# Projected values in a graph kernel: shifted to their key places by the stores instead of by matmuls

## The chip, the cores and the metric

The kernel runs on one core of one Trainium2 chip. The metric is the device time of one execution in microseconds, the median of three runs; lower is better. TensorE (PE) does matrix products, VectorE (DVE), ScalarE (ACT) and GpSimd (POOL) work elementwise, and SyncE (SP) does nothing but issue transfers. Transfers issued by SP run on the queue q1, those issued by POOL on the queue q0; both use the same 16 DMA engines.

## The reference, cut to what matters

A graph of 3327 tokens with 128 features and a dense adjacency matrix `adj` (3327 x 3327) passes through four layers, each of them a message step, the residual sum and a layer norm. Only the first is touched here, an attention that uses `adj` as additive encoding:

```
n, d = x.shape                       # 3327, 128;  h = 8
q = (x @ Wq.T).reshape(d, n, h)      # the same for k and v
a = jnp.einsum('dnh,dmh->dnm', q, k) * scale
a = a + spatial_encoding + edge_encoding          # both are adj
a = jax.nn.softmax(a, axis=2)
out = jnp.einsum('dnm,dmh->dnh', a, v)
out = out.reshape(n, h * d)
return out @ Wo.T
```

There are 128 attention problems ("heads" d) with 3327 queries, 3327 keys and only 8 features. The reshape does not split features: it reads the projected matrix as one flat row. Value m of head d stands at flat place d * 3327 + m (in units of 8 numbers), so it comes from token (d * 3327 + m) // 128 and channel (d * 3327 + m) % 128. Because 3327 = 26 * 128 - 1, a key m = 128 * s + j of head d has channel (j - d) modulo 128 and token 26 * d + s, or one token less when j < d. The other three layers multiply `adj` (once also its transpose) with the features and are the same in both kernels.

## The kernel before, in words

The program has three parts.

The opening (lines 256 to 406, to some 300 us) projects the tokens. Tokens go in seven passes u of up to 512 (`SUPER`). `split` makes the query or key products of a pass on PE (`products`, L300, four groups of 128 tokens, 1024 columns each), cuts each number into a high part on ACT (L354) and a rest on DVE (L355), takes the largest on DVE (L357), and POOL stores both parts in the DRAM scratch `q_s` or `k_s` (L294). The tiles `hi` and `lo` have two buffers each, which queries and keys of a pass use in turn. Into the same loop go the transposes of later weights (`later_weights`) and, in passes 1 to 4, one row tile of the adjacency each (`ar`, loaded by SP at L89, its maxima on DVE at L403).

For the values, `values_projected` (L312) multiplies a pass of tokens by the value weights of each of the 8 features h: the result has one channel per partition and one token per column, and is copied by DVE and ACT in turn to `vp` (contiguous per h). Attention wants value m of a head on partition m % 128, and the channel is off by d. So `values_turned` (L321) handles two heads at a time: it multiplies the 26 tokens of the head by a 128-column window of `turn`, an identity with a zero block on each side; the window that starts at column 128 + r moves partitions by r, and a second product with the window at r brings in those that wrap around, from the next token. These products (L336) add up in PSUM, a strided copy (L159 on DVE, L157 on ACT, in turn) puts them in `vo`, and after 16 heads SP stores `vo` in the scratch `v_img` (L345) by four stores, one for each key block. `v_img` has 128 rows, one per partition of keys, and is laid out in each row by key block, then by group of four heads, head, token and feature, so that what attention loads at once is contiguous. `vo` shares its two buffers (tag `wide`) with the row tile `ar`.

Attention (L410 to 850, to some 9740 us) runs over 28 blocks, 7 of 476 queries by 4 of keys (7, 7, 6 and 6 tiles of 128 keys, `KBS`), and in each block over the 32 groups of four heads. PE makes the scores (L737), ACT their exponentials (L742) and, for a fixed share, DVE by a polynomial (L631 to L641); PE weighs the values (L777). The order on PE, ACT, POOL and DVE is written out by a planner in Python with costs per step; SP's order, and that of all engines in the opening, is the framework's. At the start of group n, `prepare` loads values for group n + 1 (`load_values`, L543) and queries and keys for group n + 2 (`load_heads`, L485). Every second call of `load_values` brings the values of two groups by one SP transfer (`vs`, L547); each call has POOL spread them (L551) into one of three padded tiles `v_pad`, 32 columns for 8 features. The products with these values come while the scores of group n + 2 are made.

The last part (from L1142) makes the other three layers and reads the attention result from the scratch `o_s` (L1255, 128 x 9 runs of 512 bytes each).

Of the kernel before, what the change touches and what calls it, by code (L numbers as in the profile page):

```python
# [10 lines left out]
F32 = mybir.dt.float32  # L11
# [8 lines left out]
P = 128  # L20
GROUP = 4
PACK = 3
SUPER = 512
# [28 lines left out]
def kernel(ctx: ExitStack, tc: tile.TileContext, x, adj, wq, wk, wv, wo,  # L52
# [14 lines left out]
    nc = tc.nc  # L67
    N, D = x.shape
    HD = wq.shape[0]
    H = HD // D  # L70
    T = (N + P - 1) // P
# [23 lines left out]
    def flat_ap(dram, at, pattern):  # L95

        f = dram.rearrange("r c -> (r c)")
        if isinstance(at, int):
            base = f[at:at + 1]
        else:  # L100
            base = f[ds(at, 1)]
        return bass.AP(base.tensor, base.offset, pattern)

    const = ctx.enter_context(tc.tile_pool(name="const", bufs=1))
    scratch = ctx.enter_context(tc.tile_pool(name="scratch", bufs=1, space=DRAM))

    ident = const.tile([P, P], F32, name="ident")
# [5 lines left out]
    q_s = scratch.tile([2 * H, RS], F32, name="q_s")  # L113
    k_s = scratch.tile([2 * H, RS], F32, name="k_s")

    v_img = scratch.tile([P, T * HD], F32, name="v_img")

    o_s = scratch.tile([A1, SLOTS], F32, name="o_s")

# [35 lines left out]
    def copy(i, dst, src):  # L155
        if i % 2:
            nc.scalar.copy(dst, src)  # L157
        else:
            nc.vector.tensor_copy(dst, src)  # L159
# [96 lines left out]
    with tc.tile_pool(name="pw", bufs=1) as pw, tc.tile_pool(name="pa", bufs=2) as pa, \  # L256
# [3 lines left out]
        def spread(u):  # L260
            base = u * SUPER
            n = min(SUPER, N - base)
            R = (n + P - 1) // P
            return base, R, n // R, n % R

        xT = pw.tile([P, NU, 4, P], F32, name="xT")
        xN = pw.tile([P, NU * SUPER], F32, name="xN")
        wqT = load_by_h(pw, ppw, wq, "wqT")
        for u in range(NU):
# [4 lines left out]
            for a, n in ([(0, P)] if full == P else [(0, 112), (112, full - 112)]):  # L274
                nc.sync.dma_start(out=xr[a:a + n, 0:R, :],
                                  in_=flat_ap(x, (base + R * a) * D, [[R * D, n], [1, R * D]]))
            if rest:
                nc.sync.dma_start(out=xr[full:full + 1, 0:rest, :],
                                  in_=flat_ap(x, (base + R * full) * D, [[D, 1], [1, rest * D]]))
            ps = pps.tile([P, 4, P], F32, tag="ps", bufs=3, name="xtr")  # L280
# [4 lines left out]
            if u == 0:  # L285
                wkT = load_by_h(pw, ppw, wk, "wkT")
                wvT = load_by_h(pw, ppw, wv, "wvT")
# [9 lines left out]
        def products(u, r, w):  # L297
            pp = pps.tile([P, HD], F32, tag="pp", name="pp")
            for c in range(0, HD, 512):
                nc.tensor.matmul(pp[:, c:c + 512], lhsT=xT[:, u, r, :], rhs=w[:, c:c + 512], start=True, stop=True)  # L300
            return pp.rearrange("p (h j) -> p h j", h=H)
# [2 lines left out]

        turn = pw.tile([P, 3 * P], F32, name="turn")
        nc.gpsimd.memset(turn, 0.0)
        nc.gpsimd.tensor_copy(turn[:, P:2 * P], ident)
        vp, vo = {}, {}  # L310

        def values_projected(u):  # L312
            n = spread(u)[1] * P
            vp[u] = pa.tile([P, H, SUPER], F32, name="vp")
            for h in range(H):
                ps = pps.tile([P, SUPER], F32, tag="ps", bufs=3, name="pv")
                nc.tensor.matmul(ps[:, 0:n], lhsT=wvT[:, h * D:(h + 1) * D], rhs=xN[:, u * SUPER:u * SUPER + n],
                                 start=True, stop=True)
                copy(h, vp[u][:, h, 0:n], ps[:, 0:n])

        def values_turned(d):  # L321

            g, i = d // 16, d % 16
            if i == 0:
                vo[g] = pa.tile([P, 4, T, 32], F32, tag="wide", name="vo")
            ps = pps.tile([P, 2, H, T], F32, tag="ps", bufs=3, name="vtr")
            for k in range(2):
                q, r = (d + k) * N // D, (d + k) * N % D
                for wrap in range(2 if r else 1):
                    at = q + wrap  # L330
                    while at < q + wrap + T:
                        u = at // SUPER
                        n = min(q + wrap + T, (u + 1) * SUPER) - at
                        s = at - q - wrap
                        first = (0 if wrap else P) + r
                        nc.tensor.matmul(ps[:, k, :, s:s + n], lhsT=turn[:, first:first + P],  # L336
                                         rhs=vp[u][:, :, at - u * SUPER:at - u * SUPER + n],
                                         start=(k == 0 and wrap == 0 and s == 0), stop=True,
                                         skip_group_check=True)
                        at += n  # L340
            copy(d // 2, vo[g][:, i // 4, :, i % 4 * H:(i % 4 + 2) * H].rearrange("p s (k h) -> p k h s", k=2), ps)
            if i == 14:
                for k0, nt in KBS:
                    w = nt * 32
                    nc.sync.dma_start(out=flat_ap(v_img, k0 * HD + g * 4 * w, [[T * HD, P], [w, 4], [1, w]]),  # L345
                                        in_=vo[g][:, :, k0:k0 + nt, :].rearrange("p g s c -> p g (s c)"))

        def split(u, w, s, top, f):
            hi = pa.tile([P, H, 4, D], F32R, tag="hi", name="hi")
            lo = pa.tile([P, H, 4, D], F32R, tag="lo", name="lo")  # L350
            R = spread(u)[1]
            for r in range(R):
                pp = products(u, r, w)
                nc.scalar.activation(hi[:, :, r, :], pp, AF.Copy, scale=f)  # L354
                nc.vector.scalar_tensor_tensor(lo[:, :, r, :], pp, f, hi[:, :, r, :].bitcast(F32),  # L355
                                               ALU.mult, ALU.subtract)
            nc.vector.tensor_reduce(top[:, u:u + 1], hi[:, :, 0:R, :].bitcast(F32), AX.XYZ, ALU.max,  # L357
                                    apply_absolute_value=True)
            store_slots(nc.gpsimd, s, 0, u, hi.bitcast(F32))
            store_slots(nc.gpsimd, s, H, u, lo.bitcast(F32))  # L360
# [25 lines left out]
            nc.sync.dma_start(out=klead_s[row:row + 1, :], in_=one)  # L386
        nc.sync.dma_start(out=k_s[:, SLOTS:RS], in_=zero[0:2 * H, :])

        d = 0
        for u in range(NU):  # L390
            split(u, wqT, q_s, top_q, SCALE / 2)
            split(u, wkT, k_s, top_k, 1.0)
            values_projected(u)
            if 2 <= u <= 4:
                later_weights(u - 2)
            last = u * SUPER + spread(u)[1] * P
            while d < D and (d + 1) * N // D + T < last:
                values_turned(d)
                d += 2
            if 1 <= u <= 4:  # L400
                ar = pa.tile([P, NP], F32, tag="wide", name="ar")
                load_rows(nc.sync, ar[:, 0:N], adj, u - 1)
                nc.vector.tensor_reduce(tops[:, u - 1:u], ar[:, 0:N], AX.X, ALU.max)  # L403
            if u == 4:
                store_tops(pw, 0, tops, P)
        assert d == D

    def attention():  # L410
        with tc.tile_pool(name="ed", bufs=1) as ed, tc.tile_pool(name="kq", bufs=3) as kq, \
# [131 lines left out]
            def load_values(b, g):  # L543
                k0, nt = KBS[blocks[b][1]]
                if g % 2 == 0:
                    pairs[b, g // 2] = kq.tile([P, 2, 7 * 32], F32, name="vs", bufs=2)
                    nc.sync.dma_start(out=pairs[b, g // 2].rearrange("p a c -> p (a c)")[:, 0:2 * nt * 32],  # L547
                                      in_=flat_ap(v_img, k0 * HD + g * nt * 32, [[T * HD, P], [1, 2 * nt * 32]]))
                vs = pairs[b, g // 2].rearrange("p a c -> p (a c)")[:, g % 2 * nt * 32:(g % 2 + 1) * nt * 32]
                vp = v_pads[(b * NHG + g) % 3]  # L550
                nc.gpsimd.tensor_copy(  # L551
                    vp[:, 32:32 + nt * GROUP * 32].rearrange("p (x c) -> p x c", c=32)[:, :, 0:H],
                    vs.rearrange("p (x c) -> p x c", c=H))
                return vp

            heads, values, pairs, edges, es, stores = {}, {}, {}, {}, {}, []
# [581 lines left out]
    wide = nc.values_load(flag[0:1, 0:1], min_val=0, max_val=1)  # L1138
# [27 lines left out]
    for i in range(4):  # L1166
        k = len(range(i, T, 4))
# [134 lines left out]
    with tc.manual_schedule(engines={mybir.EngineType.PE, mybir.EngineType.SP, mybir.EngineType.DVE}):  # L1302
# [21 lines left out]
        for t in range(T):  # L1324
            n = tokens(t)
            ps = gather(t, y1, 0, 6 + t % 2,
                        after(xs[1], t - 1, messages) if t else
                        [(2 + 5 * k, lambda k=k: stage0(T + k)) for k in range(4)])
            z = work.tile([P, D], F32, name="z")
            nc.vector.tensor_tensor(z[:n, :], ps[:n, 0:D], y1[:n, t, :], ALU.add)  # L1330
            h = work.tile([P, D], F32, name="h")
# [28 lines left out]
        for t in range(T):  # L1360
            n = tokens(t)
# [9 lines left out]
            ps = gather(t, y2, 0, 7 - t % 2, [(6, back)] + after(xs[0], t - 1, last_inputs))  # L1371
            h = work.tile([P, D], F32, name="h")
# [42 lines left out]
```

## Time and profile before

| | |
|---|---|
| time, median of 3 runs | 10480.76 us (10480.22 to 10483.09) |
| the profiled execution's own time | 10484.38 us |
| its span | 10482.6 us |
| PE, ACT, DVE, POOL busy over the span | 99%, 90%, 87%, 15% |
| transfers over the span | 2226.20 MB in 1017515 packets, mean 212 GB/s |
| 0 to 330 us: PE, DVE, ACT busy | 269.46, 190.60, 110.35 us |
| 0 to 330 us: the turning products L336 on PE | 97.52 us |
| first score product L737 | at 321.99 us |

The profile lists, for one execution, what each engine did and when. Groups of instructions carry the line of the kernel, the engine, the operation, the tiles written and read, the count, the busy time and the mean duration; a bracket behind a line of the timeline tells how long the engine had stood idle and what ended that. A matmul on 32-bit floats shows as two records. The table of stretches gives each engine's busy time in a window (with the number of instructions), TensorE's granted clock (1.00 is full speed), the mean busy share of the 16 DMA engines and the rate. The table of queues gives packets, megabytes and the time of the packets as a share of 16 engines over the window.

### The profile page before, as it was taken

The page shows a single profiled execution, that of the slowest core. Times are in us where ns is not written, and L with a number is a line of the kernel's source. Part 1 is how long each engine was busy: PE and PEld are TensorE (multiplying, and loading weights), DVE is VectorE, ACT ScalarE, POOL GpSimd, SP SyncE. Part 2 cuts the span into 40 slices and gives each one's busy share as a digit, 9 for nine tenths or more (in the row PEclk, how much of TensorE's full clock was granted, in tenths as well). Part 3 has the DMA queues.
Part 4 walks back from the last instruction along what each step waited for, and adds up shares of the span by engine and source line. Part 5 has one row for each costly group of instructions (what it writes and reads, how often), then busy time and mean ns, then how long its engine had stood idle before and what let it go on. Part 6 is the DMA issues. An engine that isn't in the chain of part 4 may idle for free. (4 is left out here: it accounts for less than half of the span.)

```text
span 10482.6 us, 208701 instructions
## 1 busy us (share of the span) xinstructions
PE 10365.6 (99%) x76835; PEld 4039.4 (39%) x76835; DVE 9079.7 (87%) x16616; ACT 9441.7 (90%) x11231; POOL 1525.6 (15%) x2733
## 2 busy tenths in 40 slices
PE   8899999999999999999999999999999999999999
PEld 5333333333333333333333333333333333333879
DVE  6789998899989999898998989989899988999722
ACT  3799999999999999999999999999999999999400
POOL 0111222111121111211112110111111210001200
PEclk9999999999999999999999999999999999999999
DMA  7766776666776667766676666666766766666786
GB/s 265 229 213 190 218 221 216 212 195 204 217 214 213 196 202 214 215 212 200 204 213 212 214 198 194 207 207 209 206 196 208 214 216 198 186 197 199 230 293 248
DMA packets 1017515, 2226.20 MB, mean 212 GB/s; under 512 B 195813, under 2 KB 720365, under 8 KB 1002671
## 3 DMA queue, kind: packets, MB, share of 16 engines
q1 hardware_dynamic: 935638, 2094.76, 65.4%
q0 software_dynamic: 79136, 116.02, 3.4%
q8 instruction: 621, 10.17, 0.4%
q14 instruction: 400, 3.28, 0.1%
q10 hardware_dynamic: 1720, 1.97, 0.1%
HBM read 1863.16 MB, written 348.72 MB: 211 GB/s over the span
## 5 line engine op out<-in xcount | busy, mean ns | idle before, releaser
L742 ACT ACTIVATE e<-sc 128x952 f32<-128x952 f32 (+2 forms) x10752 | 9220.3, 995 | 219.7 <-PE sc L737 144.7
L777 PE MATMUL o<-e,v_pad 128*32 128x476 f32 (+1 forms) x46592 | 5660.4, 573 | 2.7 <-DVE e L641 1.5
L737 PE MATMUL sc<-qt,kt 64*128 64x476 f32 x23296 | 4309.5, 436 | 28.8 <-DVE ey L631 15.4
L737 PEld LDWEIGHTS sc<-qt,kt 64*128 64x128 f32 x23296 | 2134.2, 184 | 4247.4 <-ACT e L742 2602.4
L641 DVE SCALAR_TENSOR_TENSOR e<-e,ey 128x476 f32<-128x476 f32 x4116 | 2643.7, 649 | 36.5
L631 DVE TENSOR_SCALAR ey<-sc 128x476 int32<-128x476 f32 x2058 | 1341.1, 652 | 587.5 <-ACT e L742 546.1
L777 PEld LDWEIGHTS o<-e,v_pad 128*32 128x32 f32 (+1 forms) x46592 | 1032.2, 108 | 1907.1 <-issue 1791.1
L551 POOL COPY v_pad<-vs 128x192 f32<-128x192 f32 (+1 forms) x896 | 438.1, 489 | 7850.1 <-PE o L777 5624.0
L641 DVE SCALAR_TENSOR_TENSOR e<-ey 128x476 f32<-128x476 f32 x2058 | 1333.1, 651 | 28.4
L641 DVE SCALAR_TENSOR_TENSOR e<-e,et 128x476 f32<-128x476 f32 x2058 | 1327.7, 648 | 7.6
L638 DVE TENSOR_SCALAR ey<-ey 128x476 int32<-128x476 int32 x2058 | 833.8, 408 | 15.0
L635 DVE TENSOR_SCALAR et<-ey 128x476 int32<-128x476 int32 x2058 | 832.9, 408 | 12.0
L242 POOL DMA_DIRECT2D adjT_s<-at x1352 | 755.1, 567 | 93.5 <-DMA adjT_s<-at 49.3
L1241 PE MATMUL bank<-y,eT 128*128 128x128 f32 (+1 forms) x4056 | 470.7, 275 | 0.4 <-DVE h L1373 0.4
L1241 PEld LDWEIGHTS bank<-y,eT 128*128 128x128 f32 (+1 forms) x4056 | 467.5, 192 | 3.3 <-DVE h L1373 0.6
L1195 ACT ACTIVATE rstd<-mv,eps 128x1 f32<-128x1 f32 x104 | 30.6, 295 | 268.6 <-DVE mv L1193 268.5
L537 DVE CAST qt<-qt 64x1904 fp32r<-64x1904 f32 x224 | 258.4, 1154 | 7.4
L791 DVE TENSOR_TENSOR acc<-o,acc 128x476 f32<-128x476 f32 x231 | 151.1, 654 | 106.2 <-PE o L777 104.7
L535 DVE TENSOR_SCALAR qt<-qt 32x1428 fp32r<-32x1428 f32 x224 | 205.9, 919 | 18.2 <-DMA qt<-lead_s 9.5
L799 POOL DMA_DIRECT2D o_s<-acc x304 | 182.8, 605 | 30.4 <-DVE acc L791 9.5
L1354 PE MATMUL bank<-a,y 128*128 128x512 f32 (+2 forms) x364 | 145.5, 562 | 0.0
L354 ACT ACTIVATE hi<-pp 128x1024 fp32r<-128x1024 f32 x52 | 53.1, 1025 | 89.8 <-PE pp L300 88.2
(142 smaller groups left out, 2231.8 us busy)
## 6 DMA issues: line engine op xcount, KB each, us to landing
qt<-qimg SPq DMA_DIRECT2D x672, 952.0 KB
kt<-k_s SPq DMA_DIRECT2D x5316, 96.0 KB
kt<-k_s SPq DMA_DIRECT2D x1762, 128.0 KB
qimg<-qt SPq DMA_DIRECT2D x224, 952.0 KB
eT<-adjT_s SPq DMA_DIRECT2D x78, 1664.0 KB
vs<-v_img SPq DMA_DIRECT2D x224, 224.0 KB
adjT_s<-at POOLq DMA_DIRECT2D x1352, 32.0 KB, 3.7
vs<-v_img SPq DMA_DIRECT2D x224, 192.0 KB
```

Of the source, the lines that this page charges most:

```text
L242: nc.gpsimd.dma_start(out=flat_ap(adjT_s, (t * P + 32 * q) * NP + c * PIECE, [[NP, 32], [P, ns], [1, P]]), in_=at[32 * i:32 * i + 32].rear ...
L535: return [(0.9, lambda: nc.vector.tensor_scalar(qt[32:64, 1:], qf[0:32, 0:GROUP - 1], -1.0, None, ALU.mult)), (0.42, lambda: nc.vector.ten ...
L537: (1.17, lambda: nc.vector.tensor_copy(qt[64:128], qf[0:64]))]
L551: nc.gpsimd.tensor_copy(vp[:, 32:32 + nt * GROUP * 32].rearrange("p (x c) -> p x c", c=32)[:, :, 0:H], vs.rearrange("p (x c) -> p x c", c=H))
L631: nc.vector.tensor_scalar(yi, x, -58 * math.log(2.0), 2 ** 24 / math.log(2.0), ALU.max, ALU.mult)
L635: nc.vector.tensor_scalar(parts["t"].bitcast(I32), yi, UPPER, EXPONENT, ALU.bitwise_and, ALU.bitwise_xor)
L638: nc.vector.tensor_scalar(yi, yi, LOWER, QUARTER, ALU.bitwise_and, ALU.bitwise_or)
L641: nc.vector.scalar_tensor_tensor(e, e if i else y, POLY[i], parts["t"] if i == len(POLY) - 1 else y, ALU.add, ALU.mult)
L737: nc.tensor.matmul(s[:, i, 0:CW], lhsT=kt[64 * rg:64 * rg + 64, k, pos * P:(pos + 1) * P], rhs=qt[64 * rg:64 * rg + 64, k, :], start=False ...
L742: nc.scalar.activation(e[:, 0:own, :], s[:, 0:own, 0:CW], AF.Exp, bias=-2 * PHASE, scale=2.0)
L777: nc.tensor.matmul(o[32 * j:32 * j + 32, 0:CW], lhsT=values[b, g][:m, c:c + 32], rhs=es[b, g * GROUP + j, r][:m, :], start=first and u == ...
L1241: nc.tensor.matmul(ps[:n, 0:D], lhsT=e[:m, s, :n], rhs=y[:m, s, col:col + D], start=(s == 0), stop=(s == T - 1))
```

## The change

The shifted identity, its products, `vp` by passes of 512 tokens and `vo` go. A pass of values now covers 19 heads (`SPAN`, the last one 14), that is 19 * 26 tokens and one more ahead of them, and `vp` holds token by token with the 8 features inside, so that the 26 tokens of one head are a contiguous run of 208 numbers in each partition. Two SP stores per pass carry these runs to `v_img`: partition p of head d goes to row p + d, and what wraps goes by the second store to row p + d - 128, taken from one token earlier. Each store takes whole sets of 32 partitions, so some runs are stored twice, once to a row outside the 128; for these `v_img` has a margin of 64 rows on both sides. The rows are now laid out by head, token and feature. A load of attention therefore takes eight separate runs per partition, one for each head, in place of one, and POOL's spreading copy swaps the order of heads and tokens. In the pass loop the values now stand ahead of the queries.

```diff
-    v_img = scratch.tile([P, T * HD], F32, name="v_img")
+    MARGIN, SPAN = 64, 19
+    v_img = scratch.tile([P + 2 * MARGIN, T * HD], F32, name="v_img")
...
-        turn = pw.tile([P, 3 * P], F32, name="turn")
-        nc.gpsimd.memset(turn, 0.0)
-        nc.gpsimd.tensor_copy(turn[:, P:2 * P], ident)
-        vp, vo = {}, {}
...
+        def values_projected(i):
+            d0 = i * SPAN
+            n = min(SPAN, D - d0)
+            at = T * d0 - 1
+            skip = 1 if at < 0 else 0
+            vp = pa.tile([P, SPAN * T + 1, H], F32, name="vp")
             for h in range(H):
                 ps = pps.tile([P, SUPER], F32, tag="ps", bufs=3, name="pv")
+                w = n * T + 1 - skip
+                nc.tensor.matmul(ps[:, 0:w], lhsT=wvT[:, h * D:(h + 1) * D], rhs=xN[:, at + skip:at + skip + w],
                                  start=True, stop=True)
-                copy(h, vp[u][:, h, 0:n], ps[:, 0:n])
-        def values_turned(d):
...
+                copy(h, vp[:, skip:skip + w, h], ps[:, 0:w])
+            row = T * HD
+            j = min(P, (P - d0 + 31) // 32 * 32)
+            nc.sync.dma_start(out=flat_ap(v_img, (MARGIN + d0) * row + d0 * T * H, [[row, j], [row + T * H, n], [1, T * H]]),
+                              in_=vp[0:j, 1:1 + n * T, :].rearrange("p (d s) h -> p d (s h)", s=T))
+            j = (P - (d0 + n - 1)) // 32 * 32
+            d = max(d0, 1)
+            nc.sync.dma_start(out=flat_ap(v_img, (MARGIN + j + d - P) * row + d * T * H,
+                                          [[row, P - j], [row + T * H, d0 + n - d], [1, T * H]]),
+                              in_=vp[j:P, (d - d0) * T:n * T, :].rearrange("p (d s) h -> p d (s h)", s=T))
...
-        d = 0
         for u in range(NU):
+            values_projected(u)
             split(u, wqT, q_s, top_q, SCALE / 2)
             split(u, wkT, k_s, top_k, 1.0)
-            values_projected(u)
...
-                    nc.sync.dma_start(out=pairs[b, g // 2].rearrange("p a c -> p (a c)")[:, 0:2 * nt * 32],
-                                      in_=flat_ap(v_img, k0 * HD + g * nt * 32, [[T * HD, P], [1, 2 * nt * 32]]))
+                    nc.sync.dma_start(
+                        out=pairs[b, g // 2].rearrange("p a c -> p (a c)")[:, 0:2 * nt * 32].rearrange("p (j c) -> p j c", c=nt * H),
+                        in_=flat_ap(v_img, MARGIN * T * HD + g * GROUP * T * H + k0 * H,
+                                    [[T * HD, P], [T * H, 2 * GROUP], [1, nt * H]]))
...
-                    vp[:, 32:32 + nt * GROUP * 32].rearrange("p (x c) -> p x c", c=32)[:, :, 0:H],
-                    vs.rearrange("p (x c) -> p x c", c=H))
+                    vp[:, 32:32 + nt * GROUP * 32].rearrange("p (t j c) -> p j t c", j=GROUP, c=32)[:, :, :, 0:H],
+                    vs.rearrange("p (j t c) -> p j t c", j=GROUP, c=H))
```

More of the change, by code (lines that the diff above doesn't have):

```diff
@@ L301, in products @@
             return pp.rearrange("p (h j) -> p h j", h=H)
-        turn = pw.tile([P, 3 * P], F32, name="turn")
-        nc.gpsimd.memset(turn, 0.0)
-        nc.gpsimd.tensor_copy(turn[:, P:2 * P], ident)
-        vp, vo = {}, {}
-        def values_projected(u):
-            n = spread(u)[1] * P
-            vp[u] = pa.tile([P, H, SUPER], F32, name="vp")
+        def values_projected(i):
[4 more added lines that the diff above has]
+            vp = pa.tile([P, SPAN * T + 1, H], F32, name="vp")
@@ L315, in values_projected @@
             for h in range(H):
                 ps = pps.tile([P, SUPER], F32, tag="ps", bufs=3, name="pv")
-                nc.tensor.matmul(ps[:, 0:n], lhsT=wvT[:, h * D:(h + 1) * D], rhs=xN[:, u * SUPER:u * SUPER + n],
+                w = n * T + 1 - skip
+                nc.tensor.matmul(ps[:, 0:w], lhsT=wvT[:, h * D:(h + 1) * D], rhs=xN[:, at + skip:at + skip + w],
                                  start=True, stop=True)
-                copy(h, vp[u][:, h, 0:n], ps[:, 0:n])
-        def values_turned(d):
[L323 to L346, printed above, removed]
@@ L387 @@
         nc.sync.dma_start(out=k_s[:, SLOTS:RS], in_=zero[0:2 * H, :])
-        d = 0
+        assert N == T * P - 1 and NU * SPAN >= D and SPAN * T < SUPER
         for u in range(NU):
+            values_projected(u)
             split(u, wqT, q_s, top_q, SCALE / 2)
             split(u, wkT, k_s, top_k, 1.0)
-            values_projected(u)
             if 2 <= u <= 4:
                 later_weights(u - 2)
[L396 to L399, printed above, removed]
             if 1 <= u <= 4:
@@ L405 @@
                 store_tops(pw, 0, tops, P)
-        assert d == D
     def attention():
```

## The prediction

> **What bounds the kernel now.** I read the page first, for the whole span, and then the stretches of the opening, because the change touches the opening and the loads of attention, and nothing else.
>
> ```profile
> span 10482.6 us, 208701 instructions
> PE 10365.6 (99%) x76835; PEld 4039.4 (39%) x76835; DVE 9079.7 (87%) x16616; ACT 9441.7 (90%) x11231; POOL 1525.6 (15%) x2733
> ```
>
> Attention, from some 322 us to 9740 us, is nine tenths of the span, and TensorE, ScalarE and VectorE are all nearly full there. The transfers are not: in the window from 5000 to 6000 us the queue table has
>
> ```profile
> q1 hardware_dynamic: 95431, 202.19, 66.9%
> ```
>
> so q1 takes two thirds of the 16 DMA engines' time. The opening looks different. The table of stretches of 20 us (busy time of PE, PEld, DVE, ACT, POOL, then granted clock, DMA share, GB/s):
>
> ```profile
> 80.00:100.00 20.00, 20.00 (x98) 16.91 (x97) 12.37 (x11) 7.05 (x8) 1.77 (x2) 1.00 0.96 348
> 120.00:140.00 20.00, 20.00 (x94) 16.64 (x93) 12.19 (x12) 6.94 (x8) 1.77 (x2) 0.91 0.76 279
> 160.00:180.00 20.00, 20.00 (x90) 15.48 (x89) 15.32 (x15) 7.82 (x9) 1.78 (x2) 0.97 0.77 286
> 200.00:220.00 20.00, 18.92 (x60) 11.30 (x61) 17.52 (x14) 6.68 (x9) 2.66 (x3) 0.86 0.50 184
> 220.00:240.00 20.00, 18.94 (x78) 13.19 (x77) 8.58 (x11) 7.46 (x12) 0.00 (x0) 1.00 0.95 329
> ```
>
> Neither PE nor the DMA engines are full throughout: they take turns. The timeline shows how. A run of 82 turning products holds PE for 14.5 us, the next query products come only behind it, and GpSimd, which issues the q and k stores, waits for them:
>
> ```profile
> 167.84 14.56 PE L336 MATMUL vtr<-vp,turn 128*128 128x208 f32 x82
> 192.47 0.89 POOL L294 DMA_DIRECT2D q_s<-hi  x1 [22.08 <-ACT hi L354]
> ```
>
> In slices of 5 us the DMA share then falls to 0.19 (165 to 170 us), 0.00 (210 to 215) and 0.25 (255 to 260), and is 1.00 or more in the slices in which two stores are queued (170 to 185). So the opening is bound by a chain: products, the store, a hole in the transfers while PE turns values.
>
> ```profile
> q0 software_dynamic: 12960, 50.32, 52.8%
> q1 hardware_dynamic: 18518, 22.49, 26.5%
> ```
>
> These are the queues from 46 us (the first k store) to 305 us, when the last value store has landed and attention's own loads and memsets start. 79.4% with the instruction queue's 0.1%: 259 x 0.794 = 205.7 us of full transfer, and 53 us of holes.
>
> **The change, part by part.**
>
> *Turning products gone.* L336 is busy 97.5 us (534 records); their 64 copies take 27.8 us of DVE and 28.2 us of ACT. PE in the first 330 us falls from 269.5 to 172 us. The memset and copy of the shifted identity (0.42 and 0.28 us on POOL near 1 us) lay beside the first loads: nothing.
>
> *Projected copies become strided.* The 56 projecting matmuls stay, 495 instead of 512 columns wide: nothing. Their copies write every eighth word. The contiguous 128x512 copy takes 683 ns on DVE, 583 ns on ACT; bounds for a strided one are these and the two strided rows, xN (16 bytes apart, 1084 ns on ACT for 512) and vo (128 bytes apart, 880 ns for 416, so 1047 for 495). I take 1.0 us, as both strided rows say: 28 x 0.32 = +9 us of DVE, 28 x 0.42 = +12 us of ACT, less than the vo copies that go. DVE ends at 172 us of 330.
>
> *Stores.* Before, 32 stores with 8 x 4 x 4 x 128 = 16384 packets of 896 or 768 bytes. After, 14 stores of 832-byte runs. Partitions times d over the seven passes give 3008, 3648, 3040, 3648, 3040, 3648 and 2240 packets, 22272 in all, since a partition between the two masks is stored twice, once into the margin. Price of a packet: from 86 to 100 us, q1, then almost only v_img, has
>
> ```profile
> q1 hardware_dynamic: 1316, 1.12, 24.9%
> ```
>
> 0.249 x 16 x 14 us / 1316 = 42.4 ns. So 16384 x 42.4 / 16 = 43.4 us becomes 59.0 us: +15.6 us. The new runs go to a different row of the scratch each, four of the old ones lay side by side; no row shows that. Bounds: 36 ns (832 bytes at the 23 bytes/ns of the 4096-byte stores, 168 ns each) gives +6.7 us, 59 ns (twice the 512-byte row below) +39 us. I take 42.4, the nearest in size and direction.
>
> *The end of the opening.* Work is 205.7 + 15.6 = 221.3 us of full transfer. Is there always a store ready? One pass of queries and keys in the fourth pass runs on PE from 139.57 to 167.84 us, 28 us, already with the projecting matmuls and with the wait for the adjacency row tile (VectorE idle 5.17 us before its maximum). The transfers of a pass: 2048 packets x 168 ns / 16 = 21.5 us for q and k, 8 to 10 us for values, 5 us for the row tile in passes 2 to 5: 31 to 36 us. So transfers become the bound, and the two hi and lo buffers are what is late next: q of the next pass waits until q of this one is stored. In stretches with stores queued the share is 0.95 to 0.96 (220 to 240, 80 to 100 us). 221.3 / 0.95 = 233 us instead of 259: **26 us earlier**. Bounds: share 1.00, 38 us earlier; the present 0.794, 20 us later, if the holes have another cause. Half-speed stretches of PE (granted clock 0.50 from 155 to 160 us) cost some 2.7 us at a restart (6.32 instead of 3.6 us for eight records); two a pass make 33 us of the 28, still within 36.
>
> On SP the value stores stand ahead of the row tiles and later weights. Four v_img issues took 3 to 9.5 us when q0 was full and eight took 32. The row tile waits behind, VectorE behind that with the lo parts, k's products behind those; it eats some of the 38 us. Against that, the row tiles no longer share buffers with vo, so the first two can load in the empty slices before 46 us (10 us of transfer). I let these two cancel.
>
> *Attention's value loads.* 448 loads, from 128 runs of 1792 or 1536 bytes to 1024 runs of 224 or 192 bytes. Issue on SP: before 0.38 us; the nearest row with as many runs (128 x 9 of 512 bytes, L1255) has 0.36 us, the v_img store with 512 runs 1.14 us. Queued behind it are one query and eight key loads for the second group ahead. Groups start 10.8 us apart, so 1 us more is covered by 21 us. Landing: POOL's copy waits for vs 172 times, but its product comes two groups later, so 20 us cover that too. Transfer: before 8 packets an engine at q1's mean of 112 ns (0.669 x 16000 / 95431), 0.9 us. After, 64 an engine, bounded by 9 ns (the 4-byte signals, too small) and 29.5 ns, from the o loads of 512 bytes at 9760 to 9780 us:
>
> ```profile
> q1 hardware_dynamic: 8923, 4.45, 82.3%
> ```
>
> 64 x 29.5 = 1.9 us, so +1.0 us per two groups (21.6 us): the share goes from 0.67 to 0.72, hidden. If that cover were gone, 448 us. The Trainium skill, "DMA: Bandwidth & Descriptors" (Specifications), says that transfers under 512 bytes fall below line rate because the engine then reads, modifies and writes. No run here shows that. At twice the 512-byte price the share would be 0.81 and the sum the same.
>
> *POOL's spreading copy.* 896 copies with as many elements; the output pattern has three loops instead of two, rows still of 8. 548 and 430 ns for 224 and 192 elements. Between nothing and a doubling; a gain has no reason. I take nothing, as cost follows elements (medians near 376 and 343 ns, 1 ns each). Where a copy lies beside VectorE, that loses: L638 took 0.58 us at 4999.87 beside a copy, 408 ns on the mean. The Trainium skill, "SBUF — State Buffer" (Who interferes with whom), says the two engines take a shared port pair in turn and the second blocks; the trace agrees with these 0.17 us.
>
> **Sum.** -26 + 0 + 0 = -26 us. The profiled execution took 10484.4 us (span 10482.6), 3.6 above the median; it goes to 10458, and the median 10480.8 to **10455 us**. About 0.2% (21 us) is what can be told from no change.
>
> **Rivals.**
> - *Full gain and more.* Row tiles load early and transfers never pause: 221.3 - 10 = 211 us, 48 us earlier, 10433 us. For it: empty slices before 46 us. Against: nothing fills 0 to 25 us better than now.
> - *Gain lost in the stores.* Scattered packets at 59 ns, or value stores that hold up the row tiles: (205.7 + 39) / 0.95 = 258 us, no change, 10480 us. For it: SP held 32 us by eight stores at 66 us. Against: 42 ns held even with q0 full.
> - *Slower: VectorE behind POOL.* If the three-loop copy takes twice as long, VectorE loses another 0.13 to 0.17 us 896 times, 134 us on the mean, in a stage where it is 92% busy. With two thirds on the path: +89 - 26 = +63, 10544 us. It ends slower from 47 us, 35% of the hits. For it: the 0.17 us. Against: same elements, VectorE's small reserve.
> - *Slower: short runs fill the queue.* It decides where 64 packets take 0.9 + 0.33 x 21.6 = 8 us, 125 ns each; at 130 ns attention gains 2% or so, 10650 us. Against: 29.5 ns for 512 bytes. The page's rule on short transfers points this way, and reaches less than half of it.
>
> **How the numbers follow.** Forecast 0.62 (own range 10440 to 10472; three quarters of it below 10460), more gain 0.08, lost gain 0.12, VectorE 0.14, queue 0.04. Faster: 0.47 + 0.08 = 0.55; same: 0.15 + 0.12 = 0.27; slower 0.18. The range takes in all but the two slower cases: 10430 to 10496.
>
> **What would show it.** Right: no vtr; DMA share 0.9 or more from 60 to 265 us; the first score product (now 321.99) near 296; q1 in attention at 0.70 to 0.75; POOL copies near 376 ns; attention's length as before. Wrong: vp copies or the copy on POOL much longer, packets of the value stores over 50 ns, holes in the transfers with VectorE waiting for the row tile, or attention longer by more than 20 us.

## The result, and the profile after

| | before | after |
|---|---|---|
| time, median (lowest to highest of 7 runs) | 10480.76 us (10479.1 to 10483.09) | 10444.85 us (10438.71 to 10451.84) |
| the profiled execution's own time, span | 10484.38, 10482.6 us | 10451.84, 10450.0 us |
| first score product | 321.99 us | 299.85 us |
| first score product to the last output store's issue | 10148.8 us | 10146.6 us |
| that issue to the end of the span | 11.8 us | 3.6 us |

The ratio is 0.9967, 95% interval 0.9958 to 0.9976: 35.9 us or 0.34% faster. The profiled execution of after is 7 us above its median, the slowest of its seven. Between the two profiles 32.6 us went: 22.2 in the opening, 2.2 in attention and the later layers, 8.2 at the very end.

The page of after, its first lines:

```profile
span 10450.0 us, 207506 instructions
PE 10285.0 (98%) x76301; PEld 3949.3 (38%) x76301; DVE 9060.6 (87%) x16584; ACT 9424.9 (90%) x11199; POOL 1519.5 (15%) x2731
```

PE lost 81 us of busy time, more than twice what the kernel gained. The same five stretches of 20 us as before (busy time of PE, PEld, DVE, ACT, POOL, then granted clock, DMA share, GB/s):

```profile
80.00:100.00 20.00, 16.90 (x33) 7.00 (x33) 12.81 (x10) 8.09 (x8) 1.77 (x2) 0.83 1.05 264
120.00:140.00 20.00, 17.40 (x35) 7.40 (x36) 12.90 (x11) 9.26 (x9) 1.77 (x2) 0.82 0.67 223
160.00:180.00 20.00, 5.30 (x9) 2.52 (x10) 7.55 (x4) 2.16 (x3) 0.89 (x1) 0.57 1.00 308
200.00:220.00 20.00, 15.51 (x35) 6.14 (x33) 16.24 (x10) 8.92 (x11) 3.54 (x4) 0.91 0.99 315
220.00:240.00 20.00, 10.14 (x17) 3.77 (x17) 9.56 (x7) 4.37 (x5) 1.77 (x2) 0.83 1.03 364
```

PE was busy through nearly all of each stretch; now it stands idle for up to three quarters of one, and the DMA engines are full in four of five. The queues from 46 to 305 us, the window that carried the prediction's 205.7 us of full transfer:

```profile
q0 software_dynamic: 13055, 50.65, 54.6%
q1 hardware_dynamic: 25872, 23.77, 34.7%
```

In attention, from 5000 to 6000 us, q1 moves the same bytes with half as many packets again, and its share hardly moves (66.9% before):

```profile
q1 hardware_dynamic: 139759, 202.79, 69.2%
```

One thing differs in the opening that is neither PE nor a store: the row tiles of the adjacency. By the tile `ar`, before and then after (durations are smallest, median, largest in ns; then first and last start):

```profile
L89 SPq DMA_DIRECT2D ar<-in_adj_dram x4: 346/346/346, 102.6 to 239.4; - x4
L403 DVE TENSOR_REDUCE tops<-ar x4: 3608/3619/3619, 109.7 to 247.6; 128x1 f32<-128x3327 f32 x4
```

```profile
L89 SPq DMA_DIRECT2D ar<-in_adj_dram x4: 352/392/422, 3.0 to 27.3; - x4
L382 DVE TENSOR_REDUCE tops<-ar x4: 3580/3608/3619, 10.0 to 63.3; 128x1 f32<-128x3327 f32 x4
```

All four are issued by 27.3 us instead of one a pass, and VectorE waits 2.0 us for them instead of 13.6. The old program gave `ar` and `vo` the same two buffers, so a row tile could load only when values had been stored; without `vo` nothing holds it. What that does to the transfers, by windows:

```profile
0.00:46.00 46.00, 30.64 (x87) 15.19 (x88) 22.37 (x30) 18.55 (x28) 4.79 (x13) 0.93 0.55 188
46.00:280.00 234.00, 214.00 (x770) 138.32 (x769) 154.20 (x123) 82.08 (x101) 22.32 (x27) 0.95 0.79 284
```

are of before, and

```profile
0.00:46.00 46.00, 30.50 (x74) 14.53 (x75) 28.38 (x28) 15.79 (x23) 3.25 (x10) 0.85 0.84 315
46.00:280.00 234.00, 148.78 (x311) 60.35 (x309) 138.42 (x101) 74.93 (x82) 26.94 (x33) 0.81 0.95 305
```

of after. The first 46 us were half empty and are now 0.84 full: (0.84 - 0.55) x 46 = 13.3 us of full transfer moved out of the stretch behind. So two explanations compete for the opening: the one predicted (PE's bursts opened holes), and the row tiles.

### The profile page after: what moved, and what is told of

The parts are those of the page before. It is cut to its first block, busy times and chain, and to the rows that moved or that the text cites. A ratio compares the mean times of both kernels' runs of the same rounds, so it can differ in the third digit from the quotient of the medians.

```text
span 10450.0 us, 207506 instructions
## 1 busy us (share of the span) xinstructions
PE 10285.0 (98%) x76301; PEld 3949.3 (38%) x76301; DVE 9060.6 (87%) x16584; ACT 9424.9 (90%) x11199; POOL 1519.5 (15%) x2731
## 5 line engine op out<-in xcount | busy, mean ns | idle before, releaser
L618 DVE TENSOR_SCALAR ey<-ey 128x476 int32<-128x476 int32 x2058 | 837.5, 410 | 14.9
L513 DVE TENSOR_SCALAR qt<-qt 32x1428 fp32r<-32x1428 f32 x224 | 205.4, 917 | 12.4 <-DMA qt<-q_s 6.7
```

The source lines that it names most:

```text
L618: nc.vector.tensor_scalar(yi, yi, LOWER, QUARTER, ALU.bitwise_and, ALU.bitwise_or)
```

## The experiments

Times are medians, ratios stand against runs of before on the same chip; "end" is the stretch from the last output store's issue to the end of the span, in the profiled run.

### Bursts and row tiles, one at a time

The first kernel is after with PE's bursts put back: about as many turning products as a pass of tokens used to have (256 in all, where before has 267), on data that is at hand, without their copies and without `vo`.

```diff
+            last = u * SUPER + spread(u)[1] * P
+            while heads_done < D and (heads_done + 1) * N // D + T < last:
+                ps = pps.tile([P, SUPER], F32, tag="ps", bufs=3, name="vtr")
+                for k in range(4):
+                    nc.tensor.matmul(ps[:, 0:208], lhsT=ident, rhs=xN[:, 208 * k:208 * k + 208],
+                                     start=True, stop=True)
+                heads_done += 2
```

> The changed kernel with PE's bursts put back alone: after the keys of a pass, for every two heads that were turned there before, four float32 products of 128x208 with the identity go into a PSUM tile that nobody reads (256 products, some 90 us of PE); no copies, no other stores. Theory (the bursts made holes in the transfers, and their removal is the gain): the opening gets 15 to 30 us longer again, 10460 to 10475 us. Rival 1 (the gain came from the row tiles of the adjacency, which no longer share buffers with vo) and rival 2 (from the 56 us of vo copies off VectorE and ScalarE): within 7 us of the changed kernel, 10438 to 10452 us.

The second is before, with one buffer for the row tile alone:

```diff
-                ar = pa.tile([P, NP], F32, tag="wide", name="ar")
+                ar = pa.tile([P, NP], F32, tag="ar", name="ar", bufs=1)
```

> The kernel before with one edit: the row tile ar has a buffer of its own, so its loads and maxima can run early; values are turned by products as before. Theory (bursts): the holes stay, only VectorE's 13.6 us of waiting for row tiles and some transfer time move: 3 to 15 us faster than before, 10466 to 10478 us. Rival 1 (row tiles): most of the gain, 10445 to 10455 us. Rival 2 (copies): as before, 10478 to 10484 us.

The third is after, with the row tile held back until the value copies of its pass. Its loads are then issued at 70.8 to 172.2 us, earlier than in before (102.6 to 239.4), but VectorE waits longer for them, 27.7 us where before waits 13.6:

```diff
                 ar = pa.tile([P, NP], F32, tag="wide", name="ar")
+                nc.vector.tensor_copy(ar[:, 0:1], vps[u][:, 1, 0:1])
```

> The changed kernel with the row tiles late again: VectorE first writes one word of ar that it reads from the vp of the same pass, so the load can start only then. Theory (opening now bound by transfers): 20 us of transfer go back into the full stretch, less the 7 us by which the first k store came later (52.0 instead of 44.7 us): 5 to 15 us slower than the changed kernel, 10450 to 10460 us. Rival 1 (row tiles are the gain): 10470 to 10480 us. Rival 2: 10443 to 10447 us.

Measured, with the fourth corner, which came last (both edits of after together):

> The kernel after with both edits: the dummy turning products (256 of 128x208) back on PE, and the row tiles held until the value copies of their pass. Alone, the first gave a first score product at 289.6 us, the second at 304.6 us; before, which has both, stands at 322.0, and with its row tiles freed at 303.2. Theory 1 (the bursts and the late row tile open the holes only together: a pass lasts longer than its 31 to 36 us of transfers only if PE's 14.5 us and VectorE's wait both lie in its chain): first score between 314 and 328 us, DMA share from 46 to 280 us below 0.88, time 10470 to 10490. Theory 2 (the late row tile alone makes them, bursts never cost anything): first score 300 to 308 as in the run with late row tiles alone, time 10460 to 10472. Theory 3 (bursts pay by a higher granted clock): 288 to 298 and 10440 to 10455.

| | time (us) | ratio to before | first score | end |
|---|---|---|---|---|
| before | 10481.86 | | 322.0 | 11.8 |
| before, row tiles early | 10455.92 | 0.9975 (0.9966 to 0.9985) | 303.2 | 3.6 |
| after, bursts back, row tiles late | 10473.62 | 0.9991 (0.9982 to 1.0) | 312.7 | 12.4 |
| after, row tiles late | 10468.02 | 0.9987 (0.9978 to 0.9996) | 304.6 | 11.7 |
| after, bursts back | 10439.5 | 0.996 (0.9946 to 0.9973) | 289.6 | 3.6 |
| after | 10444.85 | 0.9967 (0.9958 to 0.9976) | 299.8 | 3.6 |

The windows of, in turn, before with early row tiles, after with bursts back, after with late row tiles, and after with both:

```profile
0.00:46.00 46.00, 28.40 (x72) 13.78 (x73) 29.39 (x28) 15.35 (x23) 3.90 (x12) 0.87 0.80 299
46.00:280.00 234.00, 225.91 (x844) 150.59 (x842) 155.62 (x132) 90.64 (x113) 28.95 (x36) 0.98 0.79 277
```

```profile
46.00:280.00 234.00, 217.87 (x823) 144.70 (x821) 141.89 (x102) 75.68 (x80) 29.52 (x37) 0.97 0.93 312
```

```profile
0.00:46.00 46.00, 29.62 (x80) 14.39 (x81) 20.86 (x27) 16.77 (x25) 3.25 (x10) 0.89 0.54 187
46.00:280.00 234.00, 142.61 (x302) 59.02 (x300) 143.81 (x105) 74.27 (x80) 26.15 (x32) 0.81 0.95 323
```

```profile
0.00:46.00 46.00, 29.94 (x81) 14.03 (x82) 21.11 (x28) 17.08 (x25) 3.26 (x10) 0.85 0.55 187
46.00:280.00 234.00, 215.98 (x789) 142.28 (x789) 146.41 (x103) 74.89 (x80) 25.48 (x31) 0.96 0.91 314
```

What follows. The one-line change to before, with every turning product, copy and store left as it was, brings 25.9 of the 36 us, 8 at the end and 18 in the opening; its time is 0.9 us above the range for the row tiles and far from the other two. Holding the tiles late costs after 23.2 us (its 10468.02 lies between the ranges of the two theories), and 34.1 when the bursts are back; some 8 of that is the end, so 15 and 25 would be the opening. The first score products of the single profiles differ by 4.8 and 23.1 us, so the smaller of the two is not well known. The bursts cost 5.6 us with late row tiles and nothing (5.4 us the other way, ranges overlapping) with early ones. Kernels that are alike in bursts and in early or late tiles still differ by 16 us (before with early tiles against after with bursts back) or 8 us (before against the fourth corner): that is the copies, the new stores and the new order together, and none of these was tried alone. In the runs with late tiles the first 46 us are at 0.54 or 0.55 again.

The window of after with bursts back is the plainest answer to the prediction: PE busy for 218 of 234 us, and the DMA share is 0.93 all the same. PE's time in turning products costs nothing there. But the holes that the prediction saw do not go with the late tiles: before with early row tiles still has a share of 0.79, and its holes come as they were described, a run of turning products, the query products behind it, and the store that waited for them. From one pass of it, a line of PE, a stretch of 5 us, and a line of GpSimd:

```profile
89.72 14.82 PE L336 MATMUL vtr<-vp,turn 128*128 128x208 f32 x84
110.00:115.00 5.00, 5.00 (x13) 2.15 (x12) 2.59 (x3) 2.52 (x3) 0.41 (x1) 1.00 0.00 0
114.58 0.89 POOL L294 DMA_DIRECT2D q_s<-hi  x1 [22.52 <-ACT hi L354]
```

The fourth corner fell between the theories: its first score, 312.7, is 1.3 us below the range for "only together" and its share, 0.91, above it, while its time lies inside that range and 1.6 us above the one for late tiles alone. So there is some interplay (late tiles cost 11 us more with the bursts there), but the tiles are the main term either way.

Why a pass cannot profit from PE's free time shows in the issue of each pass's first query store (POOL, after):

```profile
74.50 0.90 POOL L295 DMA_DIRECT2D q_s<-hi  x1 [1.85 <-ACT hi L337]
130.74 0.89 POOL L295 DMA_DIRECT2D q_s<-hi  x1 [35.62 <-ACT hi L337]
155.81 0.89 POOL L295 DMA_DIRECT2D q_s<-hi  x1 [9.64 <-ACT hi L337]
201.72 0.89 POOL L295 DMA_DIRECT2D q_s<-hi  x1 [10.62 <-ACT woT L158]
232.68 0.89 POOL L295 DMA_DIRECT2D q_s<-hi  x1 [15.59 <-ACT hi L337]
253.82 2.01 POOL L295 DMA_DIRECT2D q_s<-hi  x3 [2.20 <-ACT hi L337]
```

Five passes from the first to the last take 179.3 us, 35.9 each: the upper end of the 31 to 36 us of transfers that the prediction gave a pass. By the same rows the bursts put back give 33.8 (82.92 to 251.89), before with early row tiles 35.8 (77.35 to 256.21), and before 41.0 (71.61 to 276.75). Before with early tiles is held by PE (225.9 of 234 us busy, share 0.79), after by the transfers (0.95), and both need 36 us: two limits of nearly the same length. That would explain why closing the holes is worth so little.

### Are the transfers the limit of after, and what does a value packet cost

Every value store twice, the second time to a scratch of its own:

```diff
-            nc.sync.dma_start(out=flat_ap(v_img, (MARGIN + d0) * row + ...
+            for img in (v_img, v_two):
+                nc.sync.dma_start(out=flat_ap(img, (MARGIN + d0) * row + ...
```

> The changed kernel with every value store issued a second time, to a second scratch of the same shape that nobody reads: 22272 more packets of 832 bytes at the 47 to 53 ns that they take in the changed kernel's stores, 65 to 74 us of transfer on 16 engines. Theory (the opening is bound by transfers, 95% busy from 46 to 280 us): 55 to 80 us slower, 10500 to 10525 us. If instead the engines or the buffers of vp set the pace and the stores lie beside them: under 25 us slower, below 10470 us.

10507.52 us (10500.3 to 10516.88), ratio 1.0024 (1.0015 to 1.0033), first score at 356.9 us. Its window:

```profile
46.00:280.00 234.00, 142.47 (x297) 56.33 (x295) 128.82 (x93) 71.90 (x77) 23.05 (x27) 0.82 0.99 314
```

62.7 us above after, with PE idle for even more of the time. 22272 more packets on 16 engines: 62.7 x 16 / 22272 = 45 ns each by the medians, 41 ns by the first score product (57.1 us later). The added packets cost about what the prediction gave such a packet, 42.4 ns, with nothing hidden, so the stretch is bound by transfers.

### Other holes: the buffers of vp, and the tiles' order

`vp` has two buffers, and after shows one long wait of each copying engine for a store that frees one (17.0 us on VectorE, 21.7 on ScalarE). With three:

```diff
-            vp = pa.tile([P, SPAN * T + 1, H], F32, name="vp")
+            vp = pa.tile([P, SPAN * T + 1, H], F32, name="vp", bufs=3)
```

> The changed kernel with three buffers for vp instead of two. PE stood idle from 98 to 122 us because the copies waited for a vp buffer whose store was late. Theory (transfers bind): the transfers were full for most of that, only the hole from 120 to 135 us can close: 0 to 8 us faster than the changed kernel, 10437 to 10445 us. Rival (vp's buffers set the pace): 10 to 25 us faster, 10420 to 10435 us.

10446.09 us (10444.39 to 10453.08): the same as after, and 10 us above the range that had the buffers set the pace. Its first score product came at 290.1 us, but three profiles with the opening of after unchanged have 299.8, 298.1 and 295.5, so single profiles are not to be read closer than some 5 us. Together with the bursts:

> The kernel after with the dummy products back on PE and three buffers for vp. Each alone had its first score at about 290 us (289.6 and 290.1; after: 299.8) and medians of 10439.5 and 10446.1. If the transfers are the floor (share 0.93 to 0.96 in each) there is nothing left to add: first score 285 to 291, 10437 to 10446. If the two remove different holes (PE's slow clock, and the wait for a vp buffer), they add: first score 278 to 284, 10428 to 10436.

10451.05 us (10442.06 to 10458.14), first score at 296.3, both later than either theory had: nothing adds. Neither of these is shown to beat after; the bursts put back alone have the lowest median, 10439.5, and a range (10435.4 to 10444.28) that overlaps that of after.

Last, the row tiles released after the last token tile instead of at once:

```diff
                 ar = pa.tile([P, NP], F32, tag="wide", name="ar")
+                nc.vector.tensor_copy(ar[:, 0:1], xT[:, NU - 1, 0, 0:1])
```

> The changed kernel, with the row tiles held back until the last tile of x is transposed (one word of ar is first written from it, some 24 us in), so that they no longer stand ahead of x and of the value weights. Theory (transfers bind; the first k store moved from 44.7 to 52.0 us because of the row tiles): 2 to 8 us faster, 10437 to 10443 us. If the early loads were worth what they cost: within 2 us, 10443 to 10447 us.

10455.43 us (10452.66 to 10460.98). That is 8 us above the upper range. The first 46 us are 0.71 full, the first score product comes at 295.4, and the end takes 11.8 us. Without the end's 8 us it would stand some 2 us from after. Two of the four tiles load at 30 and 32 us, the other two only at 88 and 148, so in this profile two tiles in the half-empty part do as much for the opening as four. What each one brings was not measured.

### Attention's value loads

Doubled, the second copy into a tile that nothing reads:

```diff
+                    more = kq.tile([P, 2, 7 * 32], F32, name="more", bufs=1)
+                    nc.sync.dma_start(
+                        out=more.rearrange("p a c -> p (a c)")[:, 0:2 * nt * 32].rearrange("p (j c) -> p j c", c=nt * H),
+                        in_=flat_ap(v_img, MARGIN * T * HD + g * GROUP * T * H + k0 * H,
+                                    [[T * HD, P], [T * H, 2 * GROUP], [1, nt * H]]))
```

> The changed kernel with attention's value loads doubled: each load of 1024 runs of 224 or 192 bytes is issued once more into a tile that nobody reads. Theory (hidden behind TensorE and ScalarE): the share of q1 in attention goes from 0.69 to about 0.73 and the time stays, 10440 to 10450 us. Rival (short runs cost attention something, which the opening's gain covers up): at least 10 us slower, above 10455 us.

And in one run of 1792 or 1536 bytes a partition, with the old spreading copy. This kernel leaves out the reordering that the new layout needs, so attention weighs values that belong elsewhere; the amount of work is the same:

```diff
+                    nc.sync.dma_start(out=pairs[b, g // 2].rearrange("p a c -> p (a c)")[:, 0:2 * nt * 32],
+                                      in_=flat_ap(v_img, MARGIN * T * HD + k0 * HD + g * nt * 32, [[T * HD, P], [1, 2 * nt * 32]]))
```

> The changed kernel with attention's loads and POOL's copy in the form of before, one run of 1792 or 1536 bytes per partition and two loops; the values read are then not in the order that the stores wrote, so the output is another one, with the same amount of work. Theory (the short runs and the three-loop copy are hidden): attention takes the same, 10440 to 10450 us, POOL's copies 484 ns on the mean as before. Rival (short runs cost attention something): 10 us faster or more, below 10435 us.

Doubled: 10449.2 us (10445.97 to 10458.34), 4 above after; one run: 10443.87 (10442.61 to 10445.25), 1 below. q1 from 5000 to 6000 us, doubled and then with one run:

```profile
q1 hardware_dynamic: 190406, 212.50, 74.5%
```

```profile
q1 hardware_dynamic: 95494, 202.28, 67.0%
```

Doubling adds 50647 packets for 5.3 points of 16000 us, 16.7 ns a packet of 224 or 192 bytes. The short runs as the change made them are hidden; only at twice as many does a little show.

### The end of the program

Eight of the 36 us lie behind the last output store. GpSimd's last lines of before and of after:

```profile
10459.28 0.54 POOL L93 DMA_DIRECT2D out_dram<-res  x1 [5.28 <-DVE res L1202]
10465.08 0.54 POOL L93 DMA_DIRECT2D out_dram<-res  x1 [5.26 <-DVE res L1202]
10470.84 1.10 POOL L93 DMA_DIRECT2D out_dram<-res  x2 [5.23 <-DVE res L1202]
```

```profile
10437.77 0.54 POOL L93 DMA_DIRECT2D out_dram<-res  x1 [8.20 <-issue]
10440.65 0.54 POOL L93 DMA_DIRECT2D out_dram<-res  x1 [2.34 <-DVE res L1182]
10446.40 1.10 POOL L93 DMA_DIRECT2D out_dram<-res  x2 [5.21 <-DVE res L1182]
```

After has a pause of GpSimd ("issue": it waited for nothing that the profile shows) ahead of the third last store, where later stores make it up. Before has none there, and waits after its last store, until 10481.8 us. It looks like one pause of some 8 us whose place differs. If that place were fixed in GpSimd's stream of instructions, eight more instructions ahead of it would move the last stores across it:

```diff
-    nc.gpsimd.memset(eps, EPS)
+    for k in range(9):
+        nc.gpsimd.memset(eps, EPS)
```

> The kernel before with eight more memsets of the 128x1 tile eps on GpSimd at the start, and nothing else. From the last output store's issue to the end of the span before shows 11.8 us, after 3.6; in the records of GpSimd every profile has one pause of about 8 us, which nothing explains, at its end: after the last store where the end takes 11.8, ahead of the third last store where it takes 3.6. Theory 1 (the pause stands at a fixed place in GpSimd's stream of instructions, so that eight more ahead of it bring the last store behind it): end 3.6 us, time 10471 to 10475, first score within 3 us of 322. Rival (the end depends on what the opening or SP does): end 11.8 us, time 10478 to 10484.

> The kernel after with late row tiles, as run before (first score 304.6, end 11.8 us, 10468.0), and the same eight memsets. If the pause moves as in the theory of the run beside it, the end takes 3.6 us and the time is 10456 to 10463, so that late row tiles cost 11 to 18 us instead of 23. If the end does not move: 10464 to 10471.

Neither end moved: 10481.37 us (10477.22 to 10485.35) and 10466.34 us (10463.45 to 10471.75), ends of 11.8 and 11.7 us. A shift by eight instructions does not do it, and nothing else speaks for that theory. What the 14 profiles do show is a rule without a cause: the end takes 11.7 to 12.4 us in all six kernels whose row tiles come late or are held, and 3.6 us in all eight in which they load at once. Why tiles of the first 250 us set the end of a program of 10 ms was not found.

## Why the prediction was right, and for which wrong reasons

The forecast was 10455 us, the range 10430 to 10496; measured 10444.85, faster, 10 us below the forecast. The size of the opening's gain was nearly right (26 us predicted, 22 in the profiles), and that was luck: the part that it was put down to brings about half of it, a term that was put at nothing brings most of the rest, and 8 us came from the end of the program.

*What bounds the opening.* "A chain: products, the store, a hole in the transfers while PE turns values." The chain is in the trace, with early tiles too. The step that failed is its price: closing these holes was to bring the 26 us. With late tiles, and a longer wait for them, everything else (bursts, copies, stores and order) brought 13.8 us (10481.86 - 10468.02), with early ones 11.1 (10455.92 - 10444.85), and the bursts alone 5.6 or nothing. The wait for the row tile was quoted (5.17 us of VectorE) but counted within a pass of 28 us and not followed to its buffer.

*"I let these two cancel."* The second failure, and where the main term hid. On SP the value stores ahead of the row tiles were to eat some gain, and the tiles' freedom from `vo` was to give 10 us back. In fact the tiles are issued by 27 us, ahead of every value store, so the first of the two does not exist; the second is 26 us in before alone (18 in the opening, 8 in the end). All four tiles load early, not the first two: 13.3 us of transfer moved forward by the windows, and VectorE's waiting for them fell from 13.6 to 2.0 us.

*The rival "full gain and more"* named this mechanism, at 48 us and a chance of 0.08, and set against it that nothing fills 0 to 25 us better. The share of 0.84 to 46 us answers that. Its 48 us were too many, since passes then hit the 36 us of their transfers.

*Turning products and copies gone.* The 97.5 us went, but the page has only 81 us less for PE: the key, query and value products of the opening rose from 163.0 to 174.5 us while the granted clock fell. It was worth little by itself. What the change brings beside the tiles, 11 to 14 us, is the bursts, 56 us of copies on VectorE and ScalarE, the new stores and the new order together. PE's time in the bursts accounts for 6 us at the most; the rest was not split further.

*Projected copies.* Taken at 1.0 us; the medians are 1046 and 1054 ns:

```profile
L160 DVE COPY vp<-pv x28: 807/1046/1067, 49.2 to 209.4; 128x495 f32<-128x495 f32 x20, 128x494 f32<-128x494 f32 x4, 128x365 f32<-128x365 f32 x4
L158 ACT COPY vp<-pv x28: 815/1054/1066, 49.8 to 206.1; 128x495 f32<-128x495 f32 x20, 128x494 f32<-128x494 f32 x4, 128x365 f32<-128x365 f32 x4
```

*Stores.* 42.4 ns a packet; measured 41 to 45 at the margin, so as a price it held. The scattered packets themselves last 39 ns in the median but 53 on the mean, past the 50 that was named as a sign of being wrong. Their times overlap where much is queued (the shares of 1.05 and 1.03 above), so their sum overstates the work. The lower bound was a little off: 4096 bytes in 168 ns are 24 bytes a ns, which gives 34 ns, not 36.

*The end of the opening.* "Transfers become the bound" and the share of 0.95 are as measured; so is "the two hi and lo buffers are what is late next" (to write `hi`, ScalarE waited 17.7 us for stores that free it, VectorE 19.0 us for `lo`). The tile `vp` was late too: 17.0 us on VectorE and 21.7 on ScalarE, each once, and cost nothing that a third buffer gave back. The 221.3 us of work cannot be read off directly: from 46 to 305 us q0 and q1 took 89.3% of 259 us, 231 us, without the tiles, with value packets at 53 ns on the mean, and with attention's first loads.

*Attention.* The share was to be 0.70 to 0.75; it is 0.69. The added time is 2.3 points of 21.6 us, 0.5 us in two groups, where 1.0 was taken: a packet of 224 or 192 bytes costs 16.7 ns, not 29.5, and the 1792-byte packet that went took 89 ns on the mean in the trace of before, not 112. The Trainium skill, "DMA: Bandwidth & Descriptors" (Specifications), counts 512 bytes as the least that reaches line rate; per byte the trace agrees, with 13 bytes a ns for these packets against 17 for the 512-byte ones, but at 0.69 of the queue it costs nothing here. Attention and what follows took 10148.8 us before and 10146.6 after.

*GpSimd's copy.* Nothing was taken, and nothing came: 373 ns in the median, its waits for `vs` a little up (1795.2 us in 172 times before), none passed on.

```profile
L531 POOL COPY v_pad<-vs x896: 341/373/3635, 306.8 to 9691.3; 128x224 f32<-128x224 f32 x90, 128x192 f32<-128x192 f32 x90
...
DMA vs<-v_img: 2032.6, 184
```

VectorE's polynomial step kept its mean (L638 408 ns before, as L618 410 ns after), so the rival that had VectorE lose 134 us did not come. Beside a copy of GpSimd that step does lose: 505 ns on the mean against 402 elsewhere before, 497 against 403 after; but only 128 and 146 of its 2058 instructions lie beside one. Nor did the rival of a full queue come. Its sum was a little high: 130 ns a packet makes the loads 1.3% longer than the two groups, not 2%, and twice the 512-byte price gives a share of 0.80, not 0.81.

*The end* was in nobody's sum. Without its 8 us the kernel would stand at 10453, two below the forecast.

## What to carry to other kernels

Where a removed tile shared its buffers with another, the change also frees the other's load: look up who has the same tag, and when that load could start, before costing the arithmetic. An engine that is busy during a hole in the transfers may cause the hole, and freeing it may still be worth little; put the work back on its own and see what time it costs. And when two limits of a stage are nearly equal, as PE and the transfers at 36 us a pass here, taking away one of them is worth only the small difference.

## What the runs showed of the hardware

- PE's granted clock fell from 0.95 to 0.81 (46 to 280 us) when the turning products went, and was 0.97 when they were put back. The Trainium skill, "TensorE: Matmul & The Clock Gate" (Part 1), says that the clock gate is set by how busy PE has been recently; the trace agrees, 0.57 in the stretch where PE was busy 5.3 of 20 us. Products put back, with the higher clock that came with them, changed the time by less than the ranges tell apart (10439.5 against 10444.85 us, early tiles); the clock alone was not tested.
- Scattered loads of 224 or 192 bytes cost 16.7 ns a packet while q1 was two thirds busy, and scattered 832-byte stores 41 to 45 ns when the engines were full.
- The end of the program took 3.6 or 11.7 to 12.4 us, by how early tiles loaded 10 ms before. The cause stays open.
